# When the open routing chains of a mixture-of-experts layer are moved on: behind every second piece, not once a round

## The chip, the cores and the metric

The kernel runs on one core of a Trainium2 chip. Its engines are TensorE (PE in the profile; its weight loads are PEld), VectorE (DVE), ScalarE (ACT), GpSimd (POOL) and SyncE (SP). Each takes its instructions in order from its own queue. The metric is the device time of one execution in microseconds (us).

## The reference

Four layers run one after the other on 4096 tokens of 128 features (64 sequences of 64, regrouped by each layer), all in float32. Cut to what matters:

```python
x = L0(x, ctx)    # relative-position attention (16 heads) + feed-forward, two layer norms
x = L1(x, ctx)    # self attention, cross attention, feed-forward, each with a layer norm
x = L2(x, ctx)    # gated fusion of two inputs, layer norm
# L3:
q = ln(x);                x = x + mha(q, q)
qc, kv = ln(x), ln(ctx);  x = x + mha(qc, kv)
h = ln(x)                                  # the last norm
logits = h @ rw.T + rb                     # router, 8 experts
vals, idx = top_k(logits, 2); gates = softmax(vals)
h1 = gelu(h @ fc1[e].T + fc1_b[e])         # 128 -> 512
eo = h1 @ fc2[e].T + fc2_b[e]              # 512 -> 128
x = x + sum over the two chosen experts of gate * eo
```

## The kernel before, in words

The tokens are cut into eight groups of 512 (four blocks of 128 tokens each). The first layer is written out by hand and kept in program order. All later layers are Python generators: `self1`, `cross1`, `forward1`, `layer2`, `self3` and `cross3` each take one group `g` through one phase and give up control (`yield`) after every piece. `drive` holds the list `running` and goes round it: in each round every running generator is moved on by one piece, new generators are admitted (attention phases with a lag of four rounds, light ones of two), and at the end of the round the generator `fill`, which is `experts()`, is moved on by one piece, or by two or three once the last exponential of the attentions has been emitted. The order in which the pieces are emitted is the priority by which a scheduler then sets the order of instructions on each engine. It also weighs its own model of when operands are ready, so that the final order on an engine isn't just the order of emission.

All instructions pass through one helper, so that nearly all of them have line 74 in the profile; they are told apart by tile names.

The last phase is `cross3(g)` (from line 1251). Its attention consists of projections, score products `sc`, a maximum `mx`, a subtraction `s`, an exponential on ACT, transposes and products `av` with the values, a division (`rec`, `o`) and an output projection `tok` which is added to `x`. Behind that comes a chain of small passes for the group:

- the last norm: `normalise` takes statistics on VectorE (`st`, `mv`, `rs`), a power on GpSimd (`rs<-rs,nhalf`), then `nmr` on VectorE and four scaled copies on ACT, into the tile `zx`, which has four buffers and also carries four columns of routing data;
- four transposes `tr<-ident,zx`, a copy to `hT` on ACT (tile `T`), the logits `pl`;
- `router`: on VectorE two rounds of maximum and choice (`lg`, `top`, `cand`, `ci`, `hot`), the difference of the two logits with an exponential on ACT (`e2`), a product `pr` that ranks the tokens within each expert, running bases from group to group (`before`, `base`, `endbase`), the routing columns of `zx` (`zx<-tok` the first of them), and the target rows `to`. GpSimd then issues eight indirect DMAs per group, `hrows<-zx,to`, which scatter the rows to the regions of their experts in DRAM. Last come the gates, turned on TensorE (`pgt`), and the product with the experts' output biases, `tok<-fc2b`, added to `x`.

`experts()` works in two halves, `PARTS = (5, 3)` groups, with 47 and 31 blocks of 128 rows. For each half `table(h)` works out on VectorE, from the counts of the experts, which block belongs to which expert (`cnt`, `cmp`, `nb`, `cum`, `past`, `eb`, `table`, and a product `pb` on TensorE for the biases). It waits in Python until the half's groups are routed:

```python
        while done["routed"] < PARTS[0]:
            yield
        yield from table(0)
        while not done["exponentials"]:
            yield
```

Then the blocks follow in a software pipeline: `load` (SyncE's `km<-hrows`, which waits for all scatters of the half to land), `turn` (transposes `xt`, scaled copy `vp` on ACT, masks and target rows `tob` on VectorE), `first` (product `f<-fcw,vp`, copied by VectorE), `hidden_turned` (transposes `ht`, four gelus on ACT), `second` (product `f<-fcw,s`, scaled by VectorE, scattered by GpSimd as `yrows<-km,tob`). At the end, and behind the first half in between, the rows are read back and summed (`o`, `out`).

Of the kernel before, what the change touches and what calls it, by code (L numbers as in the profile page):

```python
# [33 lines left out]
ROWW = D + 4  # L34
# [60 lines left out]
def kernel(ctx: ExitStack, tc: tile.TileContext, a: dict, out: bass.AP):  # L95
# [16 lines left out]
    def wtile(shape, tag, bufs, dtype=F32):  # L112
        if tag in COMMON:
            return pools["common"].tile(shape, dtype, tag=tag, bufs=COMMON[tag], name=tag)
        return pools["work"].tile(shape, dtype, tag=tag, bufs=bufs, name=tag)
# [4 lines left out]
    def extra(name):  # L120

        return pools["psx"].tile([P, 512], F32, tag="extra", name=name)
# [15 lines left out]
    def v3(ap, n):  # L138
        return ap.rearrange("p (a b) -> p a b", a=n)

    def last(ap, n):

        return ap.unsqueeze(2).to_broadcast([ap.shape[0], ap.shape[1], n])

    def mid(ap, n):

        return ap.unsqueeze(1).to_broadcast([ap.shape[0], n, ap.shape[1]])

    def drive(phases, lags, ends, fill):

        todo = {kind: [] for kind in lags}
        for n, (start, kind) in enumerate(phases):
            for g in range(NG):
                todo[kind].append((n, g, start))

        todo["light"].sort(key=lambda task: task[1])
        passed = {(-1, g) for g in range(NG)} - {(-1, g) for g, gen in ends}
        count = 0
        running, wait = [(-1, g, gen) for g, gen in ends], {kind: 0 for kind in lags}
        while running or any(todo.values()):
            for kind, tasks in todo.items():
                if wait[kind] <= 0:
                    for task in tasks:
                        n, g, start = task
                        if (n - 1, g) in passed:  # L170
                            tasks.remove(task)
                            running.append((n, g, start(g)))
                            wait[kind] = lags[kind] - (kind == "attention" and not todo["light"])
                            break
                wait[kind] -= 1
            for task in list(running):
                n, g, gen = task
                if next(gen, "end") == "end":
                    running.remove(task)
                    passed.add((n, g))  # L180
            count += 1
            for _ in range(2 + count % 2 if done["exponentials"] else 1):
                next(fill, "end")
        for _ in fill:
            pass

# [462 lines left out]
    def experts():  # L649
# [7 lines left out]
        def table(h):  # L657

            cnt = wtile([P, NE], "cnt", 1)
            nc.vector.tensor_tensor(cnt, endbase[h], start, ALU.subtract)  # L660
            cmp = v3(wtile([P, 512], "pT", 7)[:, 0 : NE * (REGION - 1)], NE)
            nc.vector.tensor_tensor(
                cmp, last(cnt[:, :], REGION - 1), mid(limit[:, :], NE), ALU.is_gt
            )
            nb = wtile([P, NE], "nb", 1)
            nc.vector.tensor_reduce(nb, cmp, axis=AX.X, op=ALU.add)
            cum = wtile([P, NE], "cum", 1)
            nc.vector.tensor_copy(cum[:, 0:1], nb[:, 0:1])
            for e in range(1, NE):
                nc.vector.tensor_tensor(cum[:, e : e + 1], cum[:, e - 1 : e], nb[:, e : e + 1], ALU.add)  # L670
            yield
            ns = NSLOT[h]
            counts = wtile([P, 512], "pT", 7)
            past = v3(counts[:, 0 : ns * NE], ns)
            jb, rb = (counts[:, (NE + k) * ns : (NE + k + 1) * ns] for k in range(2))
            nc.vector.tensor_tensor(past, last(index[:, 0:ns], NE), mid(cum[:, :], ns), ALU.is_ge)
            eb = wtile([P, ns], f"eb{h}", 1)
            nc.vector.tensor_reduce(eb, past, axis=AX.X, op=ALU.add)
            nc.vector.tensor_tensor(past, past, mid(nb[:, :], ns), ALU.mult)
            nc.vector.tensor_reduce(jb, past, axis=AX.X, op=ALU.add)  # L680
            yield
            nc.vector.tensor_tensor(jb, index[:, 0:ns], jb, ALU.subtract)
            nc.vector.scalar_tensor_tensor(rb, eb, float(REGION), jb, op0=ALU.mult, op1=ALU.add)

            nc.vector.tensor_scalar(rb, rb, float(NE * REGION), float(P), ALU.min, ALU.mult)
            tab = wtile([1, 2, ns], f"table{h}", 1, I32)
            nc.vector.tensor_copy(tab[:, 0, :], rb[0:1, :])
            nc.vector.tensor_scalar(
                tab[:, 1, :], eb[0:1, :], float(NE - 1), 1024.0, ALU.min, ALU.mult
            )  # L690

            hot = wtile([NE, ns], "hotb", 1)
            nc.vector.tensor_scalar(hot, eb[0:NE, :], lane[0:NE, :], None, ALU.is_equal)
            yield
            pb = extra("pb")
            for c in range(NFC):
                nc.tensor.matmul(
                    pb[:, c * ns : (c + 1) * ns], lhsT=fc1bT[:, c, :], rhs=hot, start=True, stop=True
                )
            hb = v3(wtile([P, NBLK * S], "mb", 3)[:, 0 : NFC * ns], NFC) if h == 0 else v3(room[:, used : used + NFC * ns], NFC)  # L700
            nc.vector.tensor_copy(hb, v3(pb[:, 0 : NFC * ns], NFC))
            tables[h] = tab, eb, hb
# [7 lines left out]
        def load(i):  # L710
            h, j = slot(i)
            rows_in = rin[i % 8]
            at = value(nc.sync, tables[h][0][0:1, 0, j : j + 1], NE * REGION * P)
            ld = nc.sync.dma_start(rows_in, hrows[h][bass.ds(at, P), :])
            for sc in done["scatters"][h]:
                tc.add_manual_dep(ld.ins, sc.name, LANDED, reason="all rows are in place")
            held[i] = {"in": rows_in}
# [92 lines left out]

        while done["routed"] < PARTS[0]:
            yield
        yield from table(0)
        while not done["exponentials"]:
            yield

# [5 lines left out]
        for t in range(-6, total + 3):  # L822
            h = sum(t + 6 >= at for at in LAST)
            while h < NH and done["routed"] < sum(PARTS[: h + 1]):
                yield
            if h < NH and h not in tables:
                yield from table(h)
            if t + 6 < total:
                load(t + 6)
            if 0 <= t < total:  # L830
                first(t)
            if 0 <= t - 1 < total:
                hidden_turned(t - 1)
            if 0 <= t - 3 < total:
                second(t - 3)
            if 0 <= t + 2 < total:
                turn(t + 2)

            for h in range(NH - 1):
                gl, at = divmod(t - 3 - LAST[h] - 4, 4)  # L840
                if 0 <= gl < PARTS[h]:
                    g = sum(PARTS[:h]) + gl
                    if at == 0:
                        reads[g] = read(g)
                    if at == 2:
                        summed(g, reads.pop(g))
            yield
# [8 lines left out]
    def other_layers(ends):  # L856
# [394 lines left out]
        def cross3(g):  # L1251
            x = xs[g]
            ct = ctx_of(g, 3)
            pc = transpose4(ct.rearrange("p b i -> p (b i)"))
            cz = wtile([P, T], "z", 4)
            nc.scalar.copy(cz, pc)
            yield
            kvT, qT = yield from together(
                ln_turned(cz, "ckv_g", "ckv_b", cz), ln_turned(x, "cq_g", "cq_b")
            )  # L1260
            add_row(x, obias[:, 1, :])
            yield
            ps = yield from attention(
                qT[:, :], v3(kvT[:, :], NB), in3[:, 1, 0:D], in3[:, 1, D : 2 * D], in3[:, 1, 2 * D :],
                wo3[:, 1, :], sc3, bias=1, then=(lambda: done.update(exponentials=True)) if g == NG - 1 else None,
            )
            nc.vector.tensor_tensor(x, ps, x, ALU.add)
            yield

            zx = wtile([P, NBLK, ROWW], "zx", 4)  # L1270
            yield from normalise(zx.rearrange("p k c -> p (k c)"), x, width=ROWW)
            yield
            pt = transpose4(zx.rearrange("p k c -> p (k c)"), ROWW)
            hT = wtile([P, T], "T", 4)
            nc.scalar.activation(hT, pt, AF.Identity, scale=col("moe_g"), bias=col("moe_b"))
            yield
            yield from router(g, hT, x, zx)

        def router(g, hT, x, zx):

# [220 lines left out]
```

## Time and profile before

| | |
|---|---|
| median of 10 runs (lowest to highest) | 1738.46 us (1734.64 to 1740.76) |
| the profiled execution: its own time | 1742.35 us |
| its span in the profile | 1740.6 us |
| mean granted clock of TensorE | 0.949 |
| TensorE busy | 1610.9 us, 93% of the span |
| VectorE busy | 1212.0 us, 70% |
| ScalarE busy | 992.0 us, 57% |
| GpSimd busy | 913.2 us, 52% |

The profiled execution is 3.9 us above the median of the runs. The page gives busy times; how much of an engine's time lies on the path that sets the end has to be read from the stages. In the last third the order of events is: the cross attentions of the last layer up to 1493 us, the first product of an expert at 1527.4 us, the last first-stage product of an expert at 1717.7 us, and the read-back and sums up to 1740.6 us.

### The profile page before, as it was taken

The numbers are of one execution on the slowest core, as the hardware profiler recorded it, in microseconds if no ns is written. First come the engines' busy times: TensorE is split into PE (matmuls) and PEld (weight loads), VectorE is DVE, ScalarE is ACT, GpSimd is POOL, SyncE is SP. The second block draws the span as 40 slices with busy tenths as digits, with TensorE's granted clock in tenths as the row PEclk, the third lists the DMA queues.
The fourth block names the chain that finished last, engine by engine and source line by source line (L and its number), as shares of the span: only waits on it lengthen the run. The fifth ranks groups of instructions, "written<-read, shape, count | busy, mean of one in ns | idle before, by whom it ended". The sixth has DMA issues, their size and how long they took to land.

```text
span 1740.6 us, 46242 instructions
## 1 busy us (share of the span) xinstructions
PE 1610.9 (93%) x18026; PEld 1164.1 (67%) x18026; DVE 1212.0 (70%) x3289; ACT 992.0 (57%) x2712; POOL 913.2 (52%) x875
## 2 busy tenths in 40 slices
PE   7799999999999999799999999999898997799996
PEld 4566666666666666466777676566676776667774
DVE  4567686767676767678877678668656786576663
ACT  4465555555555555346665555566777874246663
POOL 2446373737373737467777577443412243664454
PEclk9899999999999999999999999899998998589998
DMA  6756455555545446320001000000000000122143
GB/s 162 164 141 159 125 145 127 143 130 141 130 136 136 136 140 174 113 81 11 9 24 32 23 14 20 7 8 2 2 14 15 8 10 19 43 76 59 54 124 89
DMA packets 215160, 136.78 MB, mean 79 GB/s; under 512 B 38896, under 2 KB 198786, under 8 KB 214816
## 3 DMA queue, kind: packets, MB, share of 16 engines
q1 hardware_dynamic: 186880, 90.54, 20.8%
q10 hardware_dynamic: 23520, 34.75, 6.1%
q0 software_dynamic: 4544, 8.54, 1.5%
q8 instruction: 144, 2.36, 0.5%
q14 instruction: 72, 0.59, 0.1%
HBM read 66.51 MB, written 68.19 MB: 77 GB/s over the span
## 4 chain that ended last, share of the span: by engine, by line
PE 64%; DVE 15%; ACT 7%; POOL 6%; DMA 4%; issue 3%; SPq 0%; POOLq 0%; ACTq 0%; DVEq 0%
PE av L74 8%; PE proj L74 8%; PE psv L74 8%; PE f L74 6%; PE psk L74 6%; PE pt L74 6%; PE tok L74 5%; PE pbd L74 4%; DVE mx L74 3%; PE psc L74 3%; DVE s L74 3%; PE acc L74 3%; PE sc L74 3%; ACT z L74 3%; PE tr L74 2%
## 5 line engine op out<-in xcount | busy, mean ns | idle before, releaser
L74 ACT ACTIVATE s<-s,nm 128x128 f32<-128x128 f32 x512 | 198.1, 388 | 244.9 <-DVE nm L74 223.0
L74 POOL TENSOR_TENSOR s<-s,sm 128x512 f32<-128x512 f32 x128 | 130.4, 1039 | 257.9 <-DVE sm L74 257.9
L74 PE MATMUL pt<-ident,s 128*128 128x128 f32 x1536 | 213.3, 283 | 22.4 <-ACT kT L74 8.3
L74 POOL TENSOR_TENSOR s<-s,mx 128x512 f32<-128x512 f32 x160 | 164.1, 1046 | 107.0 <-DVE mx L74 106.8
L74 PEld LDWEIGHTS pt<-ident,s 128*128 128x128 f32 x1536 | 176.9, 145 | 42.8 <-issue 14.3
L74 ACT ACTIVATE pT<-pt 128x512 f32<-128x512 f32 x256 | 141.9, 605 | 75.7 <-PE pt L74 71.1
L74 POOL TENSOR_TENSOR rs<-rs,nhalf 128x4 f32<-128x4 f32 x80 | 81.4, 1018 | 187.1 <-DVE rs L74 158.3
L74 POOL TENSOR_TENSOR skew<-skew,mb 128x512 f32<-128x512 f32 x128 | 160.0, 1271 | 33.8 <-DMA skew<-scr 33.3
L74 PEld LDWEIGHTS av<-vb,pT 128*64 128x64 f32 x4096 | 132.7, 144 | 18.1 <-issue 13.7
L74 PE MATMUL av<-vb,pT 128*64 128x18 f32 x4096 | 140.4, 216 | 1.9 <-DVE vpT L74 1.8
L74 DVE TENSOR_REDUCE mx<-s 128x8 f32<-128x512 f32 x160 | 102.8, 674 | 43.3 <-ACT s L74 43.3
L74 PE MATMUL psk<-kv,wk 128*128 128x512 f32 x256 | 127.6, 621 | 0.0
L74 PE MATMUL psv<-wv,kv 128*128 128x256 f32 x512 | 127.4, 392 | 0.0
L74 POOL DMA_INDIRECT yrows<-km,tob x78 | 76.2, 977 | 86.0 <-DVE m L74 62.2
L74 PE MATMUL sc<-km,qs 32*64 32x256 f32 x2048 | 103.6, 423 | 17.1 <-ACT qs L74 13.5
L74 DVE COPY pT<-pt 128x512 f32<-128x512 f32 x128 | 82.1, 682 | 37.5 <-PE pt L74 37.5
L74 PEld LDWEIGHTS psv<-wv,kv 128*128 128x128 f32 x512 | 92.2, 189 | 15.1 <-issue 1.0
L74 PEld LDWEIGHTS av<-pT,v 128*64 128x64 f32 x2048 | 66.5, 138 | 52.8 <-issue 31.1
L74 PEld LDWEIGHTS pbd<-rT,qp 64*128 64x128 f32 x1024 | 63.0, 189 | 58.0 <-DVE qp L74 56.2
L74 DVE TENSOR_TENSOR s<-sc,mb 128x512 f32<-128x512 f32 x128 | 81.9, 680 | 27.0 <-PE sc L74 27.0
L74 ACT ACTIVATE z<-z,nmr,rs 128x128 f32<-128x128 f32 x160 | 66.1, 488 | 53.8 <-DVE nmr L74 40.1
L74 DVE TENSOR_TENSOR s<-psc,skew 128x512 f32<-128x512 f32 x128 | 87.4, 683 | 12.9 <-issue 7.3
(237 smaller groups left out, 3741.1 us busy)
## 6 DMA issues: line engine op xcount, KB each, us to landing
scr<-stage SPq DMA_DIRECT2D x64, 516.0 KB, 4.8
skew<-scr SPq DMA_DIRECT2D x128, 256.0 KB, 4.0
hrows<-pad ACTq DMA_DIRECT2D x66, 330.0 KB, 2.5
ctx<-in_ctxT SPq DMA_DIRECT2D x24, 256.0 KB, 2.6
km<-hrows SPq DMA_DIRECT2D x78, 66.0 KB, 1.8
fcw<-in_fc ACTq DMA_DIRECT2D x16, 256.0 KB, 4.5
kv<-in_xT SPq DMA_DIRECT2D x8, 256.0 KB, 4.9
kv<-in_ctxT SPq DMA_DIRECT2D x8, 256.0 KB, 5.8
```

What stands on the lines that cost most here:

```text
L74: ins = it(*args, **kw)
```

## The change

A generator can now give out the marker `CHAIN` in place of nothing. `chain(gen)` wraps a generator so that each of its yields is such a marker. `drive` keeps the set `chains` of the tasks that gave the marker last, and in `filling[0]` what `fill` gave last. In a round the tasks that are not in a chain are moved on as before; behind every second of them, and once more at the end of the round, `advance_chains` moves every open chain, `fill` too if it is in one, on by a piece. The pieces of `fill` that are not a chain (the expert blocks) each have `advance_chains` behind them. Marked as chains are both calls of `table`, and in `cross3` all that follows the attention's sum: the last norm, its transposes and the router.

```diff
+    CHAIN = "chain"
+
+    def chain(gen):
+        for _ in gen:
+            yield CHAIN
...
-        count = 0
+        count, chains, filling = 0, set(), [None]
...
+        def advance(task):
+            n, g, gen = task
+            said = next(gen, "end")
+            chains.discard(task)
+            if said == "end":
+                running.remove(task)
+                passed.add((n, g))
+            elif said == CHAIN:
+                chains.add(task)
+
+        def advance_chains():
+            for task in [task for task in running if task in chains]:
+                advance(task)
+            if filling[0] == CHAIN:
+                filling[0] = next(fill, "end")
...
+            beats = 0
             for task in list(running):
-                n, g, gen = task
-                if next(gen, "end") == "end":
-                    running.remove(task)
-                    passed.add((n, g))
+                if task not in chains:
+                    advance(task)
+                    beats += 1
+                    if beats % 2 == 0:
+                        advance_chains()
+            advance_chains()
             count += 1
             for _ in range(2 + count % 2 if done["exponentials"] else 1):
-                next(fill, "end")
+                if filling[0] != CHAIN:
+                    filling[0] = next(fill, "end")
+                    advance_chains()
...
-        yield from table(0)
+        yield from chain(table(0))
...
-                yield from table(h)
+                yield from chain(table(h))
...
             zx = wtile([P, NBLK, ROWW], "zx", 4)
-            yield from normalise(zx.rearrange("p k c -> p (k c)"), x, width=ROWW)
-            yield
+            yield CHAIN
+            yield from chain(normalise(zx.rearrange("p k c -> p (k c)"), x, width=ROWW))
+            yield CHAIN
             pt = transpose4(zx.rearrange("p k c -> p (k c)"), ROWW)
             hT = wtile([P, T], "T", 4)
             nc.scalar.activation(hT, pt, AF.Identity, scale=col("moe_g"), bias=col("moe_b"))
-            yield
-            yield from router(g, hT, x, zx)
+            yield CHAIN
+            yield from chain(router(g, hT, x, zx))
```

No operation is added or taken out: what changes is the order in which pieces are emitted, and with it the order on each engine.

## The prediction

> **What bounds the kernel now.** I read the totals and the forty slices of the page first, then the timeline of TensorE and VectorE over the last third, then the table by stage, then the timeline of GpSimd.
>
> ```profile
> PE 1610.9 (93%) x18026; PEld 1164.1 (67%) x18026; DVE 1212.0 (70%) x3289; ACT 992.0 (57%) x2712; POOL 913.2 (52%) x875
> PEclk9899999999999999999999999899998998589998
> ```
>
> TensorE is the engine to feed. Of 43.5 us each, slices 34 to 36 run at 8, 5 and 8 tenths of the clock: that is 1436 to 1566 us, where the last attentions, the routers and the table of the experts meet. The change touches nothing earlier: up to about 1368 us the two instruction orders are the same. The table by stage (stretch, length, then PE, PEld, DVE, ACT, POOL busy, clock, DMA share, GB/s):
>
> ```profile
> 1383.00:1402.00 19.00, 19.00 (x270) 14.89 (x270) 15.72 (x58) 15.53 (x32) 6.17 (x6) 0.91 0.01 2
> 1402.00:1422.00 20.00, 17.63 (x278) 13.82 (x273) 16.35 (x70) 16.14 (x34) 6.38 (x6) 1.00 0.01 2
> 1422.00:1449.00 27.00, 23.43 (x321) 18.28 (x327) 20.71 (x84) 17.84 (x36) 12.38 (x12) 0.87 0.07 22
> 1473.00:1494.00 21.00, 19.21 (x262) 17.68 (x261) 10.68 (x69) 6.25 (x13) 9.07 (x10) 0.72 0.08 28
> 1494.00:1527.00 33.00, 23.90 (x92) 18.40 (x92) 20.54 (x151) 6.05 (x15) 24.37 (x25) 0.50 0.19 57
> ```
>
> The first row is attention alone, with TensorE never idle. In the last row only 92 matmuls run, at half clock: six routers and the table, chains of short VectorE steps, are worked off with nothing beside them. That tail is what the change moves. Its ends:
>
> ```profile
> 1381.32 1.61 PE L74 MATMUL sc<-km,qs 32*64 32x256 f32 x32
> 1401.68 1.62 PE L74 MATMUL sc<-km,qs 32*64 32x256 f32 x32
> 1422.83 1.65 PE L74 MATMUL sc<-km,qs 32*64 32x256 f32 x32
> 1448.60 1.12 PE L74 MATMUL sc<-km,qs 32*64 32x256 f32 x32
> 1489.52 3.61 PE L74 MATMUL av<-vb,pT 128*64 128x18 f32 x64
> 1527.39 2.07 PE L74 MATMUL f<-fcw,vp 128*128 x2 [0.34 <-ACT vp L74]
> ```
>
> A clean period of attention is 1401.68 - 1381.32 = 20.4 us; attention ends at 1493.1, and the first expert matmul starts at 1527.39. Where chains already run, VectorE waits in order behind a write into a zx buffer whose scatter, four groups older, has not landed, and TensorE waits for VectorE (start, duration, then in brackets the idle time and its releaser):
>
> ```profile
> 1440.11 0.17 DVE L74 COPY zx<-tok 128x4 f32<-128x4 f32 x1 [5.12 <-DMA hrows<-zx,to]
> 1463.27 0.17 DVE L74 COPY zx<-tok 128x4 f32<-128x4 f32 x1 [5.06 <-DMA hrows<-zx,to]
> 1465.74 1.01 PE L74 MATMUL pgt<-ident,gates 128*8 128x128 f32 x4 [4.97 <-DVE both L74]
> ```
>
> Last, GpSimd, which computes the norm's power and issues eight scatters per group, each 0.96 us at a pitch of 1.26 us:
>
> ```profile
> 1425.19 1.01 POOL L74 TENSOR_TENSOR rs<-rs,nhalf 128x4 f32<-128x4 f32 x1 [4.99 <-DVE ci L74]
> 1426.40 1.23 POOL L74 DMA_INDIRECT hrows<-zx,to  x1 [0.20 <-DVE nmr L74]
> 1430.41 0.95 POOL L74 DMA_INDIRECT hrows<-zx,to  x1 [0.30 <-issue]
> 1431.67 0.96 POOL L74 DMA_INDIRECT hrows<-zx,to  x1 [0.30 <-issue]
> ```
>
> Here the power of the next norm comes before the scatters; nmr waits about 1 us for it.
>
> **What it removes.** No arithmetic is added or taken away; the driver emits chain pieces earlier, and each engine's order follows. In the new order, routers of groups 0 to 4 and the table lie between the last attentions, and the last attention matmul is some ten instructions ahead of the first expert matmul, where now it is 29 ahead. The tail of 1527.39 - 1493.1 = 34.3 us thus nearly goes. The two waits of 5.1 us go too: each zx<-tok now comes a full period behind the scatters it needs.
>
> **What it adds, first part.** The five TensorE steps of a chain (transposes of zx 0.44, logits 0.95, ranks 0.37, turned gates 0.45, bias product 1.08) no longer fill a tail; ranks, gates and bias, 1.9 us, are new in each attention period, the first two being there already. VectorE has room: some 13 us of attention and 8 of chain make 21 us.
>
> The new wait is on GpSimd's queue. For three groups (0, 1, 2) the order puts the power of the next group's last norm behind all eight scatters and one subtraction: 8 x 1.26 + 1.05 + 1.0 = 12.1 us from the first index. VectorE, in order, has about 5.9 us of work ahead of the nmr which needs that power: four maxima of scores (0.67 each), three subtractions (0.68), a reciprocal 0.35, the scaled output 0.35, and 0.5 of small steps. So it stands for about 6.2 us. Behind nmr are the gates' copy, the next statistics and the next residual, so TensorE runs dry: 6.2 plus 1.5 us until VectorE feeds it, 7.7 us, and there is no slack, since it was busy 19.00 of 19.00 us. A stalled period is 20.4 + 1.9 + 7.7 = 30.0 us. Groups 3 and 4 have their power ahead of the scatters.
>
> The third stalled period is shorter, 27.8 us, because no further attention starts within it. The clock comes on top. After the gap of 4.97 us above the four turned gates took 1.01 us, against 0.45 in full clock, and the stage 1422 to 1449, with gaps of up to 2.73 us, was granted 0.87, or 27 x 0.13 = 3.5 us; part of such a loss falls in idle time. I take 2 us a stall, 6 in all, bounds 0 and 18 (the 0.72 of 1473 to 1494, 5.9 us, three times).
>
> [...]
>
> Sum up to the first expert matmul. The scores now at 1381.32 start 1.9 us later, for one chain's extra products: 1383.2. Three stalled periods: 1383.2 + 30.0 + 30.0 + 27.8 + 6 = 1477.0, for what now stands at 1448.60: 28.4 us lost. From there attention needed 1493.1 - 1448.6 = 44.5 us; less the second 5.06 us wait, plus 2 x 1.9 us for two groups' chains, 43.2 us, so it ends at 1520.2. The table's index copy, the load of the first rows (3.7 us from the table at 1519.83 to landing at 1523.5) and the first transposed block (about 3.9 to 1527.39) are covered in part by the last attention; I take 6 us behind it. First expert matmul: 1526.2, against 1527.39: 1.2 us gained. The cover is the weak term: uncovered, 7.6 us; fully covered, 1 us.
>
> **What it adds, second part: behind the first expert matmul.** Now 1717.72 - 1527.39 = 190.3 us pass to the last first-stage product: 77 blocks of 2.295 are 176.7, left-over TensorE work 5.0, lost 8.6. The chains of groups 6 and 7 now run among the blocks: group 7's rank product moves from one place behind the first expert matmul to 110 behind it. Left-over work grows to 6.0 us: +1.0. Group 7's power is queued behind result scatters and earlier rows, and its nmr stands 3 to 4 us on VectorE, ahead of hidden-layer copies: +2.5, bounds 0 and 6. Two routers' exponentials fall between gelus and cost ACT four more table loads:
>
> ```profile
> L74 ACT ACT_TABLE_LOAD x2 | 2.6, 1283 | 6.0 <-DMA h<-in_wr 6.0
> ```
>
> That is 4 x 1.28 = 5.1 us on ACT, which is busy 1.6 of 2.3 us in each block; two blocks lie between a gelu and its use, so I take +1.0, bounds 0 and 5. [...]
>
> The second half's table is wanted about 41 blocks, 94 us, after the first; group 7 done 20 to 30 us later is hidden, and costs nothing until that cover is gone. SyncE's row loads wait for the same scatters, only earlier. The end behind the last block stays.
>
> Sum: -1.2 + 1.0 + 2.5 + 1.0 = +3.3 us. The profiled execution took 1742.35 us (span 1740.6), 3.9 over the median of 1738.46; 1745.7 less 3.9 is **1741.8**.
>
> **Rivals.**
>
> *The power's wait hides (faster).* If VectorE has 12 us of work ahead of nmr, or waits there for ACT and PE anyway, the three stalls shrink to their extra TensorE work: 3 x 7.7 - 2.2 + 6 = 27 us less in the sum, and 1715. With half hidden, 1728. For it: in-order VectorE had 4 us idle in each clean period, and such waits may overlap. Against it: GpSimd's 12.1 us is arithmetic on a measured pitch, and VectorE's 5.9 us are counted from rows.
>
> *The clock stays down (slower).* Three gaps of 7.7 us are longer than any gap in attention now. If each leaves the following period at the 0.72 of 1473 to 1494, 5.9 us are lost in place of 2: +11.7, 1753.5. It decides from where the gaps recur before TensorE has regained full clock. For it: that stage follows a single gap of 4.97 us. Against: the stage had weak feeding all along.
>
> *The change does not do what it says.* For groups 6 and 7 it does the reverse: their chains end among the experts. If the first table is also held up (its last scatters land about 2.3 us after issue, 12 us after group 4's index), the first expert starts where it does now, the stalls and gains cancel, and only part of the later costs remains: 1738 to 1740, no change.
>
> **How the numbers follow.** A measurement of this kernel can tell about 0.2%, 3.5 us, from no change. Forecast with own range 1735 to 1750: 0.45, of which 0.12 lies within 0.2%. Hidden wait, 1712 to 1731: 0.30. Clock, 1748 to 1760: 0.17. No change: 0.08. Faster 0.32 (with 0.02 of the forecast), same 0.19, slower 0.49. Leaving out about 0.1 at either end gives 1718 to 1755.
>
> **What would show it.** Right: successive scores some 30 us apart three times from 1383 on; nmr waiting about 6 us for rs from POOL, three times; no zx<-tok wait of 5 us; six table loads; first expert matmul near 1526; expert stretch 193 to 196 us. Wrong: first expert matmul before 1515 (the stalls hid), or after 1535 (clock or table), or an expert stretch over 200 us.

## The result, and the profile after

The changed kernel took 1770.08 us (median of 9 runs, 1761.83 to 1774.58) against 1738.47 us before (31 runs): ratio 1.0171, 95% interval 1.0158 to 1.0183. It is 31.6 us slower, where 1741.8 us was forecast and 1755 was the upper end. Its profiled execution has a span of 1770.3 us against 1740.6.

The page after, totals and granted clock in forty slices of 44.3 us:

```profile
PE 1620.3 (92%) x18026; PEld 1175.5 (66%) x18026; DVE 1207.8 (68%) x3289; ACT 999.3 (56%) x2716; POOL 914.0 (52%) x875
PEclk9899999999999999899999998899889677699998
```

The work is the same (TensorE 18026 instructions, VectorE 3289; ACT has four more, the table loads). Four slices in a row, 1372 to 1549 us, run at 6 to 7 tenths of the clock, where before three ran at 8, 5 and 8. The table by stage, at the same times as before:

```profile
1383.00:1402.00 19.00, 9.59 (x172) 8.04 (x171) 11.98 (x46) 8.43 (x17) 11.38 (x11) 0.84 0.10 31
1402.00:1422.00 20.00, 18.75 (x192) 15.44 (x192) 11.38 (x56) 13.05 (x27) 4.29 (x4) 0.73 0.00 1
1422.00:1449.00 27.00, 18.55 (x240) 16.44 (x248) 12.86 (x67) 10.73 (x22) 11.91 (x12) 0.71 0.07 22
1473.00:1494.00 21.00, 20.92 (x257) 16.84 (x256) 11.88 (x59) 9.76 (x19) 3.09 (x3) 0.72 0.01 2
1494.00:1527.00 33.00, 27.12 (x324) 23.38 (x324) 18.19 (x70) 13.48 (x27) 14.14 (x15) 0.69 0.08 25
```

Attention's first row had TensorE busy all 19.00 us; now it is busy 9.59. The stretch that was the empty tail (92 matmuls at 0.50) now holds 324 matmuls of attention and chains. But the stages ahead of it have lost more than that. The scores that mark the periods, the last attention product and the first expert product:

```profile
1384.99 1.29 PE L74 MATMUL sc<-km,qs 32*64 32x256 f32 x32
1420.33 1.50 PE L74 MATMUL sc<-km,qs 32*64 32x256 f32 x32
1456.76 1.12 PE L74 MATMUL sc<-km,qs 32*64 32x256 f32 x32
1489.33 1.64 PE L74 MATMUL sc<-km,qs 32*64 32x256 f32 x32
1543.87 3.61 PE L74 MATMUL av<-vb,pT 128*64 128x18 f32 x64 [2.36 <-DVE before L74]
1552.17 1.47 PE L74 MATMUL f<-fcw,vp 128*128 x2
1747.46 1.02 PE L74 MATMUL f<-fcw,vp 128*128 x2
```

A period is the time from one `sc` row of the first four to the next. The periods are 35.3, 36.4 and 32.6 us; the first expert product starts at 1552.17, 24.8 us later than before. The last first-stage product starts at 1747.46, so the experts' stretch is 195.3 us against 190.3. What follows is 22.8 against 22.9 us. 24.8 + 5.0 - 0.1 is the 29.7 us by which the spans differ.

VectorE's long waits and TensorE's that go with them, in the two timelines:

```profile
1400.33 0.16 DVE L74 SCALAR_TENSOR_TENSOR nmr<-mv,rs 128x4 f32<-128x4 f32 x1 [7.02 <-POOL rs L74]
1435.08 0.16 DVE L74 SCALAR_TENSOR_TENSOR nmr<-mv,rs 128x4 f32<-128x4 f32 x1 [6.81 <-POOL rs L74]
1469.88 0.16 DVE L74 SCALAR_TENSOR_TENSOR nmr<-mv,rs 128x4 f32<-128x4 f32 x1 [6.34 <-POOL rs L74]
1401.91 2.07 PE L74 MATMUL tok<-fc2b,T 8*128 8x128 f32 x8 [7.94 <-DVE T L74]
1436.66 2.07 PE L74 MATMUL tok<-fc2b,T 8*128 8x128 f32 x8 [7.73 <-DVE T L74]
1471.14 2.04 PE L74 MATMUL tok<-fc2b,T 8*128 8x128 f32 x8 [6.95 <-DVE T L74]
```

These are the three stalls that the forecast named (6.2 and 7.7 us). On GpSimd's timeline the power that ends the first is right behind the last scatter:

```profile
1398.26 0.96 POOL L74 DMA_INDIRECT hrows<-zx,to  x1 [0.30 <-issue]
1399.23 1.07 POOL L74 TENSOR_TENSOR rs<-rs,nhalf 128x4 f32<-128x4 f32 x1
```

### The profile page after: what moved, and what is told of

Its sections match the earlier page's. It is cut to its first block, busy times and chain, and to the rows that moved or that the text cites. A ratio compares the mean times of both kernels' runs of the same rounds, so it can differ in the third digit from the quotient of the medians.

```text
span 1770.3 us, 46231 instructions
## 1 busy us (share of the span) xinstructions
PE 1620.3 (92%) x18026; PEld 1175.5 (66%) x18026; DVE 1207.8 (68%) x3289; ACT 999.3 (56%) x2716; POOL 914.0 (52%) x875
## 5 line engine op out<-in xcount | busy, mean ns | idle before, releaser
L74 PE MATMUL pt<-ident,s 128*128 128x128 f32 x1536 | 217.8, 286 | 21.5 <-ACT kT L74 8.4
L74 PEld LDWEIGHTS pt<-ident,s 128*128 128x128 f32 x1536 | 181.4, 147 | 41.3 <-issue 14.3
L74 POOL TENSOR_TENSOR skew<-skew,mb 128x512 f32<-128x512 f32 x128 | 160.1, 1273 | 32.2 <-DMA skew<-scr 31.8
L74 PEld LDWEIGHTS av<-vb,pT 128*64 128x64 f32 x4096 | 138.8, 149 | 27.0 <-issue 17.5
L74 PE MATMUL av<-vb,pT 128*64 128x18 f32 x4096 | 146.6, 220 | 7.9 <-DVE before L74 4.2
L74 ACT ACTIVATION_READ_ACCUMULATOR s<-s,nm 128x1 f32 x512 | 95.6, 187 | 0.0
```

The lines of the kernel that those rows point to most:

```text
L74: ins = it(*args, **kw)
```

## The experiments

The kernel before took 1737 to 1740 us on some chips and 1766 to 1771 on two others. So each kernel is given as its ratio to the kernel before on its own chip, and ratios are set against each other only among chips of one sort, or within one group. On the two slower chips the experts' stretch takes 203 to 217 us in all eight kernels, where the others' takes 187 to 199. The traces of these eight also hold waits for which no releaser is named, the longest 11.2 us on VectorE; the others' traces hold none of over 0.2 us there. What slows these chips is not known, and the eight kernels are weak evidence.

**hold0: the stall on GpSimd taken away.** The scatters of groups 0 to 2 move to the chain's end; seven of the eight then come behind the next power.

```diff
-                for k in range(NBLK):
-                    sc = nc.gpsimd.indirect_dma_start(...)      # in mid-chain
+                tos.append(to)
+            if g >= 3:
+                scatter()                                       # the same eight scatters
...
             nc.vector.tensor_tensor(x, pb, x, ALU.add)          # end of the chain
+            if g < 3:
+                scatter()
```

> The changed kernel, but for groups 0 to 2 the eight scatters are issued at the end of the chain (behind the bias product) and not in its middle, so that on GpSimd the next group's power comes ahead of seven of them. Theory Q (the queue on GpSimd makes the three stalls of VectorE, and the gaps on TensorE they leave make the half clock): nmr waits under 2 us for rs, no TensorE gap of 7 us, second scores 21 to 24 us apart, clock 0.95 or more between 1385 and 1480, first expert matmul at 1500 to 1515, time 1720 to 1735. Rival K (the half clock comes from the short products that now lie between the attentions, not from gaps): the gaps go, 3 x 7.5 us, but the clock stays near 0.71, time 1745 to 1755. Rival L (the loss is made by table loads and chains among the experts): over 1760.

Measured: 1755.23 us, ratio 1.0101 (1.0085 to 1.0118). The three waits of 6 to 7 us are gone (the longest that is left there is 1.91 us), and about 12 us with them: the part of theory Q about the stall holds. But the periods are 30.6, 29.8 and 28.6 us, not 21 to 24, and the time is at the upper end of K's, though the clock was 0.77 to 0.82 in these periods, above K's 0.71. TensorE's timeline and the table by stage of this kernel show two smaller waits in each period, and the clock behind them:

```profile
1394.64 0.80 PE L74 MATMUL pgt<-ident,gates 128*8 128x128 f32 x4 [1.88 <-DVE o L74]
1396.20 2.07 PE L74 MATMUL tok<-fc2b,T 8*128 8x128 f32 x8 [0.77 <-DVE T L74]
...
1395.00:1405.00 10.00, 9.23 (x84) 8.20 (x82) 4.15 (x24) 2.58 (x5) 5.50 (x6) 0.50 0.09 29
1405.00:1415.00 10.00, 9.48 (x86) 7.05 (x85) 7.10 (x29) 8.79 (x18) 2.27 (x2) 0.82 0.01 2
```

**fill7, fill11 and short27: what keeps the clock.** Products that nobody reads are put into the gaps of groups 0 to 2, in the tile that the bias product overwrites.

```diff
         ps = pmm("tok")
+        for _ in range(fill):          # 7 or 11 for groups 0 to 2; short27: 27, with 8 columns
+            nc.tensor.matmul(ps, lhsT=ident, rhs=fcw[:, 0:512], start=True, stop=True)
```

> The changed kernel with seven products of 128x512 that nobody reads, put on TensorE ahead of the bias product of groups 0 to 2, where it stands idle for 7 to 8 us; VectorE's waits stay as they are. Theory Q (gaps make the half clock): the gaps on TensorE are filled, the clock between 1385 and 1500 rises from 0.71 to over 0.9, the periods of second scores shrink from 35 to about 30 us, time 1748 to 1758. Rival K (short products make the half clock): the clock stays below 0.8 and the time at 1768 to 1776.

Measured: 1764.85 us, ratio 1.0159 (1.0142 to 1.0176). This overlaps with the changed kernel's, so the gain is unclear, though the clock from 1385 to 1500 us rose to 0.85. Gaps of 3.52, 2.56 and 2.54 us were left.

> The changed kernel with eleven instead of seven unread products of 128x512 (11.3 us) in each of the three gaps of groups 0 to 2, so that nothing of a gap is left idle. Theory G (an idle spot on TensorE, not the wait of VectorE as such, costs the clock): full clock from 1385 to the end of the gap and behind it, periods of second scores of 30 to 32 us, time 1748 to 1760 where the changed kernel has 1770. Rival S (the short products behind the gap drop the clock whether or not it was idle): the clock falls behind the gap as before, periods 33 to 36, time 1764 to 1775.

Measured: ratio 1.0157 (1.0140 to 1.0174), periods 34.2, 33.7 and 28.8 us. The table by stage of this kernel:

```profile
1385.00:1420.00 35.00, 31.46 (x333) 21.93 (x331) 20.91 (x90) 19.35 (x38) 16.16 (x16) 0.90 0.06 17
1420.00:1455.00 35.00, 33.49 (x348) 24.05 (x348) 20.68 (x91) 19.55 (x38) 14.76 (x15) 0.90 0.05 17
1455.00:1490.00 35.00, 34.67 (x448) 24.61 (x446) 21.90 (x97) 18.20 (x34) 12.73 (x13) 1.00 0.05 17
```

VectorE still stands 7.00, 6.79 and 6.79 us for GpSimd. The clock is back at 0.90 to 1.00, but the 0.90 hides a split: in the first two periods it falls again behind the filled gap, at new waits of 2.28 and 1.48 us for ScalarE (0.63 from 1411 to 1419, 0.57 from 1445 to 1452). In the third period it stays at 1.00. TensorE's timeline of this kernel: first the wait of the first period, then the third period's bias product, and last the scores that end that period:

```profile
1411.73 1.87 PE L74 MATMUL pl<-rw,T 128*128 128x8 f32 x8 [2.28 <-ACT T L74]
...
1473.20 1.15 PE L74 MATMUL tok<-fc2b,T 8*128 8x128 f32 x8
...
1485.38 1.64 PE L74 MATMUL sc<-km,qs 32*64 32x256 f32 x32
```

From the bias product to these scores that is 12.18 us. The changed kernel takes 18.19 us for the same products in its third period (1471.14 to 1489.33), at a mean clock of 0.63. TensorE is never idle in either stretch, so the half clock cost 6.0 us there. All three periods together take 96.7 us against 104.3, although the added products put off the third bias product by 2.3 us. In the time as a whole the gain is not clear of noise. Theory G's clock and its price thus hold in the third period; the first two went as rival S says, but at new idle spots.

> The changed kernel with 27 products of 128x8 (about 7 us) in place of the seven of 128x512, at the same place for groups 0 to 2. Rival B (the clock counts busy time): the clock stays up into the gap as with the seven dense products, 0.85 or more between 1385 and 1490, time 1760 to 1768. Theory G, in the form that only dense products count: the clock falls some 4 us into the short products and stays at half for 12 us or more, 0.70 to 0.78 as in the changed kernel, time 1768 to 1775.

Measured on a slower chip (kernel before 1771 us): ratio 1.0279 (1.0246 to 1.0313). The products of 8 columns (each has two rows in the trace) keep TensorE busy, and the clock falls among them: it is 1.00 from 1394 to 1396 us, 0.58 in the next two and 0.50 from there on, as theory G had it. It comes back between 1416 and 1418 us, when the next projection starts (`proj`, 128x512, at 1417.06). The last row of the unread products, and the table by stage:

```profile
1394.51 8.74 PE L74 MATMUL tok<-fcw,ident 128*128 128x8 f32 x48 [0.55 <-issue]
...
1385.00:1395.00 10.00, 8.85 (x165) 7.54 (x163) 8.84 (x33) 4.01 (x9) 6.49 (x7) 1.00 0.10 30
1397.00:1416.00 19.00, 18.87 (x146) 17.25 (x153) 6.70 (x39) 6.74 (x15) 5.20 (x6) 0.50 0.04 12
1417.00:1425.00 8.00, 7.43 (x96) 5.48 (x88) 6.49 (x23) 7.27 (x14) 2.27 (x2) 1.00 0.01 2
```

**tabonly and crossonly: one half of the change each.** In tabonly the markers in `cross3` are plain yields again; in crossonly `chain(...)` is taken off both tables.

> The changed kernel, but only the two tables are chains; last norm and router are moved on once a round as before. Theory Q and rival K: no power is queued behind scatters more than before, second scores as before (20.4, 21.2, 25.8 us), first expert matmul at 1518 to 1527, time 1730 to 1739. Rival L: the chained table among the experts costs, over 1745.

> The changed kernel, but the two tables are no chains; last norm and router are. Theory Q: the three stalls of 6 to 7 us and the half clock stay, first expert matmul at 1550 to 1560, time 1766 to 1780. Rival L: 1745 or less, as the table no longer competes.

Measured: tabonly 1744.97 us, ratio 1.0042 (1.0025 to 1.0059); crossonly 1772.06 us, 1.0190 (1.0172 to 1.0209). The last norm and router as chains bring the whole loss. The tables alone cost 7 us, against the expectation: the waits for an older scatter grow from 5.1 to 6.54 and 7.51 us. The two halves don't add up to the change.

**early4, v1, bfill: late chains, turned gates, the old tail's clock.** All three on one chip. early4 is hold0 with chains for groups 0 to 3 only; v1 is hold0 with the pieces behind the scatters (gates, turned gates, bias product) no longer chained; bfill is the kernel before with two dense products ahead of the turned gates of groups 2 to 7.

```diff
-            yield CHAIN                                    # early4
+            mark = CHAIN if g < 4 else None
+            yield mark
...
+            yield FREE                                     # v1: chain() gives plain yields from here on
             gates = wtile([P, NBLK, NE], "gates", 3)
...
             pgt = extra("pgt")
+            dense(pgt, 2 if g >= 2 else 0)                 # bfill
```

> The kernel with the scatters of groups 0 to 2 at the chain's end (1755 us), and only groups 0 to 3 have chains; the chains of groups 4 to 7 move on once a round, as in the kernel before. Then no router's exponential falls between gelus (two table loads and not six). Theory: of the 17 us that the held scatters leave, half is made by late chains and the blocks' competition, so 1743 to 1750. Rival G (the clock in the attention periods makes all of it): 1752 to 1760.

> The kernel with the scatters of groups 0 to 2 at the chain's end (1755 us), and there the last pieces of each chain (gates, turned gates, bias product, for groups 0 to 2 the scatters too) are no chain but moved on once a round. Theory G: TensorE no longer stands before the turned gates and the bias product, periods of 24 to 27 us at a clock over 0.88 up to 1475, time 1735 to 1748. Rival D (VectorE's chain sets the period): as with the held scatters, 1752 to 1760.

> The kernel before, with two unread products of 128x512 ahead of the turned gates of groups 2 to 7, which run between 1465 and 1560 at half clock. Theory G: the clock of 1494 to 1527 rises from 0.50 to 0.7 or more, first expert matmul 2 to 6 us earlier, time 1731 to 1736. Rival (the tail is set by VectorE and GpSimd, and TensorE's clock there costs nothing): 1737 to 1745.

Measured: early4 1.0088 (1.0071 to 1.0105), v1 1.0087 (1.0070 to 1.0104), hold0 above 1.0101: no difference can be told, and both theories that forecast a gain missed. In early4 the experts' stretch shrinks from hold0's 192.5 to 187.3 us, but the first expert product starts 5 us later (1542.37 against 1537.32). In v1 the first period, with no wait of over 2 us for GpSimd and at a clock of 1.00, takes 24.9 us; then the wait for GpSimd's power returns (2.98, 4.70 and 6.51 us), perhaps because fewer instructions lie ahead of nmr, which was not tested. From the start of this period to the first expert product v1 takes 147.1 us against hold0's 153.2, but its experts' stretch is 199.3 us against 192.5, which takes the gain back. bfill: 1.0017 (1.0004 to 1.0029), a hair slower. Its clock in the tail rose from 0.50 to 0.70, and nothing was gained:

```profile
1490.00:1525.00 35.00, 26.12 (x134) 18.06 (x132) 22.44 (x164) 5.83 (x14) 24.38 (x25) 0.70 0.19 56
```

So the rival's forecast holds: TensorE's clock does not set that tail.

**own1, own1f, own1fe4, own2f: GpSimd out of the way.** On one of the slower chips (kernel before 1766 us). The last norm's power is worked out on VectorE; "f" adds v1's edit, "e4" early4's, own2f takes the other two norms' powers off GpSimd too.

```diff
+            nc.vector.tensor_scalar(yi, rs.bitcast(I32), 1, None, ALU.logical_shift_right)
+            nc.vector.tensor_scalar(yi, yi, -1.0, 1597463007.0, ALU.mult, ALU.add)
+            for k in range(3):
+                nc.vector.tensor_tensor(t, y, y, ALU.mult)
+                nc.vector.scalar_tensor_tensor(t, t, -0.5, rs, op0=ALU.mult, op1=ALU.mult)
+                nc.vector.scalar_tensor_tensor((y, y, rs)[k], t, 1.5, y, op0=ALU.add, op1=ALU.mult)
-        nc.gpsimd.tensor_tensor(rs, rs, nhalf, ALU.pow)
```

> The changed kernel with the last norm's power worked out on VectorE (shift, subtraction and three steps of Newton's method, 11 small operations in place of one, some 2.2 us a group) and not on GpSimd; the scatters stay in mid-chain. Theory Q+G (the stall on GpSimd is worth 15 us, the half clock and TensorE's order the rest): no wait of nmr for GpSimd in the last norm, 1752 to 1760 as with the held scatters. Rival P (GpSimd sets the pace in other ways too): under 1748.

> As own1, and the last pieces of each chain (gates, turned gates, bias product) moved on once a round. Theory G: no stall and no TensorE standing before the turned gates, three periods of 24 to 26 us (the first period of the kernel with both, v1, took 24.9 us), first expert matmul at 1515 to 1525, time 1738 to 1748. Rival D (VectorE, with 2.2 us more a group, sets periods of 28 us and more): 1752 or over.

> As own1f, and only groups 0 to 3 have chains. Theory: the experts' stretch is 187 to 190 us in place of 195 (no table loads between gelus, no late power behind result scatters), time 5 to 8 us under own1f, 1733 to 1742, near the kernel before. Rival (late routers ahead of the first expert matmul delay it by as much): equal to own1f within 3 us.

> As own1f, with the powers of the two norms ahead of the cross attention on VectorE too, 33 small operations a group in place of three. Theory P: nothing but scatters is left on GpSimd's way, 3 to 6 us under own1f. Theory D (VectorE sets the period): 3 to 12 us over own1f.

Measured: own1 1810.11 us, ratio 1.0253 (1.0219 to 1.0288); own1f 1792.45, 1.0165 (1.0126 to 1.0204); own1fe4 1786.20, 1.0114 (1.0081 to 1.0147); own2f 1786.86, 1.0122 (1.0079 to 1.0166). Against each other: taking the gates out of the chain is worth 18 us. The late chains and the other powers come out at 6 us each, but the intervals overlap, so neither can be told. own1, forecast at 1752 to 1760 beside 1738, missed by far; its trace holds unnamed waits of up to 10.7 us on VectorE and 10.8 us on TensorE. In own1f VectorE has no wait of over 2 us for GpSimd, and the periods are 32.3, 32.2 and 34.6 us, not 24 to 26. The numbers are D's, but VectorE was busy only 25.2 of 35 us there. Nor does the run refute theory G: its condition, that TensorE no longer stands before the turned gates, was not met, and the clock in the three periods was 0.74, 0.84 and 0.70. TensorE's timeline shows the wait:

```profile
1393.85 1.01 PE L74 MATMUL pgt<-ident,gates 128*8 128x128 f32 x4 [4.29 <-DVE o L74]
```

**hold0fill, beat4, beat99.** Also on a slower chip. hold0fill adds five dense products to hold0 for groups 0 to 4; beat4 and beat99 move chains on behind every fourth piece, and only at the round's end and behind the blocks (`beats % 4`, `beats % 99`).

> The kernel with the scatters of groups 0 to 2 at the chain's end (1755 us), and for groups 0 to 4 five products of 128x512 that nobody reads (1.02 us each) on TensorE ahead of the turned gates, where it stands idle for 2 to 5 us in each period and its clock drops. Theory G (what is left of the loss, 17 us, is half clock: an idle spot drops the clock and it stays down for 12 us, up to the next dense product): full clock from 1385 to 1450, periods of second scores of 23 to 26 us in place of 30, first expert matmul at 1515 to 1528, time 1732 to 1746. Rival D (VectorE's chain sets the period of 30 us, and the clock only follows it): the clock rises but the periods stay at 29 to 31 us, time 1752 to 1760.

> The changed kernel, but the open chains are moved on behind every fourth piece of the others and not every second. Theory Q: chains begin a little later, but the next power is still behind the eight scatters, so stalls of 5 to 7 us stay, time 1760 to 1775. Rival (the pace alone does the harm, a smaller pace halves it): 1748 to 1756.

> The changed kernel, but inside a round the chains are not moved on at all, only once at its end and behind every expert block. Theory Q: one power less behind the scatters, nmr stands at most 3 us, fewer routers ahead of the end of attention, first expert matmul at 1525 to 1535, time 1735 to 1750. Rival L (the blocks' own moves of the chains among the experts cost most): over 1755.

Measured: 1.0184 (1.0140 to 1.0227), 1.0260 (1.0225 to 1.0294) and 1.0206 (1.0173 to 1.0239). hold0fill is inconclusive: with the dense products VectorE's order changed, and the wait for GpSimd came back (3.75 and 2.17 us). A slower pace doesn't help clearly: in beat99 nmr still stands, twice, for about 8 us. In beat4, against its expectation, nmr waits at most 1 us for GpSimd; its loss goes with five unnamed waits of 6.1 to 11.2 us on VectorE, so it says nothing of the pace.

```profile
1457.37 0.16 DVE L74 SCALAR_TENSOR_TENSOR nmr<-mv,rs 128x4 f32<-128x4 f32 x1 [8.02 <-POOL rs L74]
```

**btok and tabtok: the removed wait alone.** The routing column that was written ahead of its turn is made to depend on the gates.

```diff
-            nc.vector.tensor_copy(meta(0), tok[:, ...])
+            nc.vector.scalar_tensor_tensor(meta(0), e2, 0.0, tok[:, ...], op0=ALU.mult, op1=ALU.add)
```

> The kernel before, with the first routing column written as 0 times the second gate plus the token numbers, so that it can't be taken ahead of the gates: the write into a buffer of zx that a scatter four groups older still reads comes some microseconds later on VectorE. Theory (VectorE's in-order wait of 5.1 us for that scatter is on the path, twice): both waits go, attention ends 5 to 9 us earlier, time 1729 to 1735 beside a kernel before of 1738 (ratio 0.994 to 0.998). Rival (the tail of routers and scatters sets the first expert matmul, and an earlier end of the attention waits there): 1737 to 1740, ratio 0.999 or more.

> The kernel in which only the tables are chains (1745 us, ratio 1.0042), with the same routing column. Theory: its waits of 6.5 and 7.5 us go, 7 to 12 us less, ratio 0.995 to 1.0. Rival: ratio 1.003 or more.

Measured: btok 1733.38 us, ratio 0.9960 (0.9945 to 0.9974), faster than both kernels; tabtok 0.9978 (0.9966 to 0.9990). In btok's timelines the column's write comes without a wait, and the first expert product starts at 1516.22, 11.2 us earlier than before; 4.0 us are given back in the experts' stretch (194.3 us).

```profile
1438.16 0.15 DVE L74 SCALAR_TENSOR_TENSOR zx<-e,tok 128x4 f32<-128x4 f32 x1
1457.20 0.17 DVE L74 SCALAR_TENSOR_TENSOR zx<-e,tok 128x4 f32<-128x4 f32 x1
1516.22 2.00 PE L74 MATMUL f<-fcw,vp 128*128 x2
```

## Why the prediction was wrong

**What held.** The three stalls came where they were named, at 7.02, 6.81 and 6.34 us (6.2 forecast), with 7.94, 7.73 and 6.95 us on TensorE (7.7). The two waits of 5 us went; btok shows alone what they were worth, 7 us in all. There were six table loads:

```profile
L74 ACT ACT_TABLE_LOAD x6 | 7.7, 1283 | 6.4 <-DMA h<-in_wr 6.3
```

The experts' stretch was 195.3 us, within 193 to 196, 5.0 us over before where 4.5 were summed. That is in part luck: fill11, hold0, fill7 and v1, also with six loads, have 195.9, 192.5, 198.6 and 199.3.

**What failed** is the sum up to the first expert product: 1526.2 forecast, 1552.17 measured, 26.0 us. By its terms: the start 1.8 us (1384.99 against 1383.2), the three periods with their clock 10.5 us (104.3 against 93.8), attention behind them 15.0 us (1489.33 to 1547.5 is 58.2, against 43.2), the last step -1.3 us (4.7 against 6).

The start is no finding: among kernels whose edits act behind that point it lies between 1380.65 (fill7) and 1388.68 (fill11). The chances were added up with a slip: by the prediction's own parts they are 0.20 for no change and 0.48 for slower, not 0.19 and 0.49.

*The step "I take 2 us a stall, 6 in all".* This is the term that failed in the stalled periods. In the changed kernel the clock did not come back soon after a gap. Its table by stage, over the three stretches behind the gaps:

```profile
1401.00:1412.00 11.00, 10.09 (x87) 9.50 (x88) 4.87 (x30) 5.24 (x12) 2.02 (x2) 0.50 0.00 1
1437.00:1452.00 15.00, 15.00 (x131) 11.90 (x131) 6.31 (x39) 7.69 (x17) 3.36 (x4) 0.50 0.01 2
1472.00:1484.00 12.00, 12.00 (x126) 10.11 (x125) 4.29 (x24) 3.85 (x7) 0.00 (x0) 0.50 0.01 1
```

That is 37.1 us of products at half clock; half of it, 18.5 us, is extra TensorE time, as an estimate from the granted 0.50, and so the upper bound of 18 and not the 6 taken. From 1437 to 1452 and from 1472 to 1484 us, 15.00 and 12.00 us of unbroken work ran at 0.50 from end to end. The rival that the clock stays down named this, but priced it at 11.7 us, on attention's periods alone. fill11's third period shows that the half clock lay on the path: at 1.00 the same work took 12.18 us and not 18.19, 6.0 us less. In the first two periods this is argued and not shown, since fill11 lost the full clock there again. As an estimate, 104.3 less 18.5 leaves 85.8 us for the three periods, where 87.8 were summed without the clock; so the stalls and the added work, taken together, were not priced too low.

*The step "VectorE has room: some 13 us of attention and 8 of chain make 21 us".* VectorE's busy time came as summed, 19.70 and 20.93 us in the first two periods. But the step also makes an unstalled period 22.3 us, as if a chain were only 1.9 us of TensorE work beside attention. The nearest case, v1's first period at full clock, took 24.9 us, 2.6 more. The turned gates stand on TensorE until VectorE has reached them (1.88 us in hold0), and the attention products behind them in order stand too. hold0's 28.6 to 30.6 us hold these waits and a clock of 0.77 to 0.82 as well; the two were not separated. So the "hidden wait" rival was too hopeful: without the stalls the time is 1755, not 1715.

*The step from the last period to the end of attention.* 44.5 us were taken over from before, with 1.9 us for each of two chains. 58.2 us here and 57.4 in hold0 (1473.03 to 1530.45) show that the loss of 15.0 us doesn't come from the stalls. From before to after, TensorE's busy time in this stretch rose from 38.6 to 46.9 us and its idle time from 5.9 to 11.3, at a mean clock of 0.80 and then 0.66. Two routers and the table now lie between the last attention products. How much of the loss is half clock and how much is one engine waiting for the other was not separated, and the cause of this part stays open.

## What to carry to other kernels

When small dependent chains are pulled into a busy stage, count for each queue what will stand behind every step that waits, and price the clock of the work behind each gap (here 37.1 us of it ran at 0.50); the sum of busy times can fall far short of the period (here VectorE was busy 19.70 us in a period of 35.3). Look first for the one early write or wait that blocks an in-order engine, as in btok: a single dependency gained 7 us where reordering the whole stage lost 30. And ask whether an engine's clock or gap lies on the path at all, before paying to mend it: bfill raised the clock from 0.50 to 0.70 for nothing, in a tail where TensorE was idle a quarter of the time; fill11's third period, where TensorE was never idle, gained 6.0 us by it.

## What the runs showed of the hardware

In these runs TensorE's granted clock did not follow busy time alone. In short27 (one run, on a slower chip) it fell to 0.50 among products of 128x8 that ran back to back, and stayed there up to 1416 us (18.87 us busy in 19.00 from 1397 on; from 1403 on these are the chain's and attention's own products). In fill11, with products of 128x512 in the same place, it was 1.00 (10.00 us busy in 10.00, from 1395 to 1405). In the changed kernel it rose again between 1412 and 1414, 1452 and 1454, and 1484 and 1486 us, where scores start at 1413.02, 1447.83 and 1482.16 and projections at 1414.07, 1449.77 and 1484.10; in short27 between 1416 and 1418 us, with scores at 1415.30 and a projection at 1417.06.

One pair of stretches ran the same mix of short products at two clocks, each at the one it began with. From 1472 to 1484 us the changed kernel ran it at 0.50, busy 12.00 of 12.00 us; fill11 ran the same products in its third period, within 1473.20 to 1485.38 us, at 1.00, having come to them at 1.00. There the clock stayed full, and here 12.00 us of the mix did not restore one that had fallen. Which part of the mix decides is not shown.
